# Two norm roots by way of ScalarE's Sqrt, one LoRA step instead of two, and token sums in parts, in a gated FFN with an S4 branch

## The chip, the core and the metric

The kernel runs on one core of a Trainium2 chip. A core has five engines that run their own instruction streams, each in order: TensorE (PE; its weight loads are listed as PEld), VectorE (DVE), ScalarE (ACT), GpSimd (POOL) and SyncE (SP), which here issues nearly all DMAs. Engines wait for one another by semaphores. SBUF is the working memory with 128 partitions, PSUM holds the results of TensorE in eight banks of 128x512 floats. The metric is the time of one execution on the device in microseconds (us): median of three runs, 442.49, from 442.27 to 443.13.

## The reference, cut to what matters

The input is x, 2 x 1024 tokens of 512 values. All is fp32.

```python
x = L0_attn_u                                   # (2, 1024, 512)
xn = _layernorm(x)                              # (x - mean) / sqrt(var + 1e-5)
s = S4(xn)                                      # a causal convolution along the 512 values of each token
g = silu(FFN(xn))                               # below
return x + s * g

# FFN, HID = 1376, R = 16, SCALING = 2
h1 = xn @ w1.T + (xn @ A1.T @ B1.T) * SCALING
h3 = xn @ w3.T + (xn @ A3.T @ B3.T) * SCALING
g  = silu(h1) * h3
out = g @ w2.T + (g @ A2.T @ B2.T) * SCALING
```

## The kernel before, in words

**Tiling.** The 2048 tokens are four blocks of 512 (`TB`), each of four tiles of 128 tokens (`NTT`); blocks 0 and 1 make "super block" 0, blocks 2 and 3 super block 1. A tile is normalized with tokens on the partitions, transposed on TensorE, and copied by ScalarE out of PSUM into `xr` and `b12`, with the 512 values (in four chunks of 128) on the partitions.

**Fast matrix products.** The first stage, h1 and h3, takes the 1376 hidden values in five pairs of 256 and a last chunk of 96 (`LAST`). w1 and w3 are first merged with their LoRA part, w + 2 B A: a product of 16 rows on TensorE (`lora_product`, L380) and an addition on VectorE (`merge`, L391). The stage is then a Strassen-Winograd product on two levels for the pairs and one level for the last chunk: seven products instead of eight per level, at the price of sums of weights and tokens. The outer sums of tokens are made by `outer_token_sum` (L328), those of weights by `outer_weight_sums` (L440); the inner ones by `inner_token_sum` (L340 makes T3, L342 T2, L344 T4, L346 T1) and `inner_weight_sum` (L452). Each inner token sum is made in two calls: `raw` over the three blocks of `xr`, 128x1536, and once over the four of `xt`, 128x2048. T2 builds on T3 and T4 on T2; T1 overwrites its operand.

**Chains.** `Chain` (L765) runs one set of seven products; `step(i)` issues product i (L755) into banks x, y or w of PSUM, and what follows it: the copy of x to w (L793), snapshots of x (L775), totals (L779). A pair's seven chains (`pair_chains`) have the inner index j = 1, 2, 6, 7, 5, 3, 4, and read T2 in j = 6 and T1 in j = 5 and T4 in j = 4. Their results are added up in `ua` and `u3` (L869), passed through Silu on ScalarE (L828), multiplied on GpSimd (L836) and stored to DRAM.

**Order of work.** The order on TensorE, VectorE, ScalarE and GpSimd is written out by hand. `at(place, what)` puts a step on a heap, `after(delay, what)` puts one behind the current place, and the heap is emptied in order of place; each engine executes its instructions in the order in which they were emitted. One unit of place is about one product. A chain's products stand at 7n plus the offsets of a table, such as `PLACES`. PSUM is given out by `bank(tag)`: x, y, w and aux have two banks each and take turns; with `borrow` the next bank is used without the turn passing.

**The start.** SP and ScalarE issue the loads of block 0; then come the LoRA factors for two row groups (`load_lora`, groups 0 and 1), block 1, the last chunk's weights, pair 0's weights, blocks 2 and 3, pair 1's weights, and the LoRA factors for groups 2 and 3. In the trace eight DMAs are under way at most: an issue starts once the one eight places ahead of it has landed. ScalarE loads the table for Silu with a dummy activation (L972). TensorE multiplies the identity by itself (`keep_warm`, L988) and makes the LoRA product of the last chunk. VectorE makes mean and variance of each tile (`norm_stats`, L247 and L248). `norm_root` (L278) adds EPS and calls `rsqrt` (L50), eight instructions on VectorE that begin with an integer guess, and makes the shift (L284); `normalize` applies both, two tiles on ScalarE (L293) and two on GpSimd (L297). Block 0 is transposed into the aux banks (L304), block 1 into the y banks. Block 3's sums are made by ScalarE (`act_sums`, `act_squares`), and one root serves blocks 2 and 3 (`norm_root(mv_late, 2, 3)`).

**LoRA of pair 0.** `merge_pair` (L407) takes half a pair at a time, four products with 16 rows in row groups 0 and 1, at places -9 and -3.8. The other pairs use `merge_whole_pair` (L418), eight products in four row groups and four banks, which needs the LoRA factors of groups 2 and 3.

After the first stage come the S4 matrix and the second stage, which the change does not touch.

Of the kernel before, what the change touches and what calls it, by code (L numbers as in the profile page):

```python
# [12 lines left out]
F32 = mybir.dt.float32  # L13
# [36 lines left out]
def rsqrt(nc, pool, v, shape):  # L50


    y = pool.tile(shape, F32, tag="rs_y", name="rs_y")
    t = pool.tile(shape, F32, tag="rs_t", name="rs_t")
    part = 3.0 / 8.0
    c2 = part * 0.703952253
    nc.vector.tensor_scalar(
        y.bitcast(I32), v.bitcast(I32), -0.5, float(0x5F1FFFF9), ALU.mult, ALU.add
    )
    nc.vector.tensor_tensor(t, y, y, ALU.mult)  # L60
    nc.vector.scalar_tensor_tensor(t, t, -c2, v, ALU.mult, ALU.mult)
# [46 lines left out]
def s4_gated_ffn(  # L108
# [110 lines left out]
    def after(delay, what):  # L219
        at(now[0] + delay, what)  # L220
# [54 lines left out]
            norms[b][:, :, 1], sums_of_x[b][:, 2, :], 1.0 / DIM, None, mult  # L275
        )

    def norm_root(mv, *blocks):  # L278
        n = len(blocks) * NTT
        veps = small.tile([P, n], F32, tag="veps", name="veps")  # L280
        nc.vector.tensor_scalar(veps, mv[:, :, 1], EPS, None, add)
        rstd = rsqrt(nc, small, veps, [P, n])
        shift = small.tile([P, n], F32, tag="shift", name="shift")
        nc.vector.scalar_tensor_tensor(shift, mv[:, :, 0], -1.0, rstd, mult, mult)  # L284
        for n, b in enumerate(blocks):
            norms[b] = [t[:, n * NTT : (n + 1) * NTT] for t in (rstd, shift)]
# [9 lines left out]
            else:  # L296
                nc.gpsimd.tensor_scalar(t, t, rstd[:, one], shift[:, one], mult, add)  # L297

    def transpose(b, tiles, tag="aux"):
        sb, low = divmod(b, 2)  # L300
        for tt in tiles:
            ps = bank(tag)
            for dc in range(NDC):
                nc.tensor.transpose(  # L304
                    ps[:, dc * P : (dc + 1) * P],
                    x_in[b][tt][:, dc * P : (dc + 1) * P],
                    ident,
                )
            at_ = slice(tt * P, (tt + 1) * P)
            halves = ps.rearrange("p (c k t) -> p c k t", c=2, k=2)  # L310
            if low == 0:
                nc.scalar.copy(xr[:, 0:2, sb, :, at_], halves)
            else:
                nc.scalar.copy(b12[sb][:, :, at_], halves[:, 0])
                nc.scalar.copy(xr[:, 2, sb, :, at_], halves[:, 1])
# [16 lines left out]
            nc.sync.dma_start(out=b12_dram[:, sb], in_=b12[sb])  # L332
        nc.sync.dma_start(out=i12_dram, in_=xr[:, :, 1, 0, :])

    def inner_token_sum(name, raw):
        src, lo, n = (xr, 0, 3) if raw else (xt, 3, 4)
        to = {i: t[:, lo : lo + n, :] for i, t in t_in.items()}
        b11, b21, b12_, b22 = (src[:, :, s, k, :] for s in range(2) for k in range(2))
        if name == 3:
            nc.vector.tensor_tensor(to[7], b22, b12_, sub)  # L340
        elif name == 2:
            nc.vector.tensor_tensor(to[6], to[7], b11, add)  # L342
        elif name == 4:
            nc.vector.tensor_tensor(to[4], b21, to[6], sub)  # L344
        else:
            nc.vector.tensor_tensor(b12_, b12_, b11, sub)  # L346
# [57 lines left out]
                )  # L404
        return w

    def merge_pair(c, w, half, tag="aux"):  # L407

        ps = [bank(tag), bank(tag)]
        for k in range(2):  # L410
            for v in range(2):
                n = slice(k * 2 * P, (k + 1) * 2 * P)
                lora_product(ps[v][:, n], v, 2 * half + k, PAIR_AT[c], 2 * P, k == 0)
        for v in range(2):
            to = w[:, (1, 2, 0, 3)[2 * v + half]].rearrange("p k m h -> p (k m h)")
            after(1.6 + v, lambda to=to, v=v: merge(to, ps[v]))

    def merge_whole_pair(c, w, first=None, delays=(1.15, 2.3, 4.3, 4.4)):  # L418

        ps = [first or [bank("y", True), bank("w", True)], [bank("aux"), bank("aux")]]  # L420
# [41 lines left out]
    def load_last():  # L462
        both = const.tile([P, 2, 2 * NDC * LASTR], F32, tag="w2b", name="last")
        w, s = (
            both[:, i].rearrange("p (a b h) -> p a b h", a=n, h=LASTR)
            for i, n in enumerate((2, 4))
        )
        for v, src in enumerate((w1T, w3T)):
            nc.sync.dma_start(
                out=w[:, v], in_=src[:, LAST * P :].rearrange("(dc p) h -> p dc h", p=P)  # L470
            )
        return w, s

    def lora_last():
        ps = [bank("y"), bank("y")]
# [487 lines left out]

    x_in = {0: load_x(0)}
    warm = const.tile([P, 1], F32, name="warm")
    nc.gpsimd.memset(warm, 0.0)
    make_identity(nc, ident)
    lora_tiles(LSPLIT)
    factors = (a1, b1T), (a3, b3T)
    for v, f in enumerate(factors):  # L970
        load_lora((nc.sync, nc.scalar)[v], v, *f, LSPLIT, HID)
    nc.scalar.activation(warm, warm, AF.Silu)  # L972
    x_in[1] = load_x(1)
    make_upper_triangular(nc, tri, 1.0, diag=True)
    w_last, s_last = load_last()
    w_pair, s_pair = {0: load_pair(0)}, {c: {} for c in range(NPAIR)}
    x_in[2], x_in[3] = load_x(2), load_x(3)
    w_pair[1] = load_pair(1)
    for v, f in enumerate(factors):
        load_lora(nc.sync, 2 + v, *f, LSPLIT, HID)  # L980

    def other_factors():
        for v, (_, h) in enumerate(factors):
# [18 lines left out]
    ps_last = lora_last()  # L1002
    mv = norm_tile(0)
    norm_stats(0, range(NTT))
    norm_root(mv, 0)
    normalize(0)

    keep_warm(primed[1], 4)
    transpose(0, range(NTT))
    mv = norm_tile(1)  # L1010
    norm_stats(1, range(2))
    merge_last(w_last, ps_last, 0)
    norm_stats(1, range(2, NTT))
    norm_root(mv, 1)
    merge_last(w_last, ps_last, 1)
    mv_late = norm_tile(2, 3)
    ab_last = last_operands(w_last, s_last)

# [37 lines left out]
            add_chain(2 + 7 * c + n, pair_chain(c, n), places)  # L1056
    at(-10, lambda: normalize(1))
    at(-9.9, lambda: last_sums(w_last, s_last))
    at(-9, lambda: merge_pair(0, w_pair[0], 0))
    at(-3.8, lambda: merge_pair(0, w_pair[0], 1))  # L1060
    for i in range(2):
        at(-6 + i, lambda i=i: transpose(1, range(2 * i, 2 * i + 2), "y"))
    for n, name in enumerate((3, 2, 1)):
        at((-2.3, -1.5, -0.45)[n], lambda name=name: outer_token_sum(0, name))
        at(-0.6 + 0.3 * n, lambda name=name: outer_weight_sums(w_pair[0], (name,)))
    at(0.4, lambda: outer_token_sum(0, 4))
    at(0.8, lambda: outer_weight_sums(w_pair[0], (4,)))
    for tt in range(NTT):
        at(-6 + 0.8 * tt, lambda tt=tt: norm_stats(2, (tt,)))
        at(-1.4 + 0.1 * tt, lambda tt=tt: act_sums(3, tt))  # L1070
        at((-0.3, -0.2, 1.7, 1.8)[tt], lambda tt=tt: act_squares(3, tt))
    at(-0.9, lambda: act_means(3))
    at(1.9, lambda: act_variances(3))
    at(6.9, lambda: norm_root(mv_late, 2, 3))
    at(7.3, lambda: normalize(2))
    at(7.7, lambda: normalize(3, (0,)))
    for n, place in enumerate((12.1, 12.8, 13.7, 14.4)):
        b, i = divmod(n, 2)
        at(place, lambda b=b, i=i: transpose(2 + b, range(2 * i, 2 * i + 2)))
# [3 lines left out]
    at(22.5, spill)  # L1083
    for name, when in ((1, 12.7), (2, 13.4), (4, 14), (3, 30.5)):
        at(when, lambda name=name: inner_weight_sum(w_pair[0], s_pair[0], name))
    for name, raw, when in (
        (3, True, 21.6),
        (2, True, 22.8),
        (3, False, 24.2),
        (2, False, 30.2),  # L1090
        (1, True, 34.4),
        (1, False, 37.5),
        (4, True, 43.3),
        (4, False, 47.6),
    ):
        at(when, lambda name=name, raw=raw: inner_token_sum(name, raw))

    for c in range(NPAIR):
        t0 = 14 + 49 * c
# [492 lines left out]
```

## Time and profile before

| what | value |
|---|---|
| median of 3 runs | 442.49 us (442.27 to 443.13) |
| profiled execution, its own time | 442.57 us |
| its span, first to last instruction | 440.8 us |
| busy TensorE / VectorE / GpSimd / ScalarE | 98% / 72% / 47% / 33% |
| mean granted TensorE clock | 0.998 |
| DMA | 53.61 MB, mean 122 GB/s |

The profile's page gives busy shares of each engine over the span, the span in 40 slices of 11 us with the busy share in tenths, and the chain of work that ended last: from the last instruction back, at each step to what released it. The timeline lists instructions in order of time: start, duration, engine, line, operation, output and inputs, and in brackets the idle time of the engine before it and what ended that. The ends of matrix products are modelled, so two that follow each other overlap in the list; the distance from start to start is what counts. Records with "x8" are several merged into one line.

### The profile page before, as it was taken

The page shows a single profiled execution, that of the slowest core. Times are in us where ns is not written, and L with a number is a line of the kernel's source. Part 1 is how long each engine was busy: PE and PEld are TensorE (multiplying, and loading weights), DVE is VectorE, ACT ScalarE, POOL GpSimd, SP SyncE. Part 2 cuts the span into 40 slices and gives each one's busy share as a digit, 9 for nine tenths or more (in the row PEclk, how much of TensorE's full clock was granted, in tenths as well). Part 3 has the DMA queues.
Part 4 walks back from the last instruction along what each step waited for, and adds up shares of the span by engine and source line. Part 5 has one row for each costly group of instructions (what it writes and reads, how often), then busy time and mean ns, then how long its engine had stood idle before and what let it go on. Part 6 is the DMA issues. An engine that isn't in the chain of part 4 may idle for free.

```text
span 440.8 us, 5156 instructions
## 1 busy us (share of the span) xinstructions
PE 433.5 (98%) x1704; PEld 268.5 (61%) x1704; DVE 316.9 (72%) x534; ACT 144.2 (33%) x296; POOL 209.3 (47%) x156
## 2 busy tenths in 40 slices
PE   7999999999999999999999999999999999999996
PEld 7545333444444444444443447888898999999995
DVE  5899999946974597469746796979786875753234
ACT  2777242453245324532453242211101212112221
POOL 2325469995689368936894469400000123222221
PEclk9999999999999999999999999999999999999999
DMA  8921304025002400350045526395902833423211
GB/s 258 370 66 47 116 0 149 24 72 168 25 24 96 143 24 25 99 160 24 25 148 187 167 90 214 112 348 200 342 22 75 306 115 95 144 97 95 88 57 48
DMA packets 35466, 53.61 MB, mean 122 GB/s; under 512 B 4688, under 2 KB 21520, under 8 KB 35312
## 3 DMA queue, kind: packets, MB, share of 16 engines
q1 hardware_dynamic: 35088, 52.69, 36.9%
q10 hardware_dynamic: 352, 0.60, 0.4%
q8 instruction: 13, 0.21, 0.2%
q14 instruction: 13, 0.11, 0.1%
HBM read 33.88 MB, written 19.40 MB: 121 GB/s over the span
## 4 chain that ended last, share of the span: by engine, by line
PE 84%; DVE 10%; issue 2%; ACT 2%; DMA 1%; POOL 0%; SPq 0%; DVEq 0%; POOLq 0%
PE x L755 42%; PE y L755 21%; PE w L755 11%; PE aux L929 4%; PE w L929 2%; DVE s L452 1%; DVE t_in L342 1%; DVE xt L328 1%; DMA s<-in_x_dram 1%; DVE t_in L340 1%; DVE w L440 1%; DVE s L779 1%; PE y L382 1%; PE y L528 1%; PE aux L710 1%
## 5 line engine op out<-in xcount | busy, mean ns | idle before, releaser
L1310 POOL TENSOR_TENSOR o<-o,xin 128x512 f32<-128x512 f32 (+1 forms) x17 | 23.3, 1369 | 132.9 <-DVE o L1309 132.9
L836 POOL TENSOR_TENSOR s<-c,s 128x512 f32<-128x512 f32 (+1 forms) x44 | 63.1, 1439 | 16.1 <-ACT c L828 10.9
L775 ACT COPY s<-x 128x512 f32<-128x512 f32 (+1 forms) x54 | 31.6, 584 | 86.8 <-PE x L755 86.7
L755 PE MATMUL x<-t_in,s 128*128 128x512 f32 (+1 forms) x148 | 55.4, 501 | 0.0
L779 DVE TENSOR_TENSOR s<-s,y 128x512 f32<-128x512 f32 (+1 forms) x54 | 36.0, 679 | 17.2 <-PE y L755 12.1
L869 POOL TENSOR_TENSOR s<-ua_three,s 128x512 f32<-128x512 f32 x20 | 35.9, 1793 | 25.7 <-DVE s L779 25.7
L755 PEld LDWEIGHTS x<-t_in,s 128*128 128x128 f32 x148 | 26.6, 190 | 23.3 <-issue 12.0
L869 POOL TENSOR_TENSOR ua_three<-ua_three,s 128x512 f32<-128x512 f32 x20 | 33.0, 1652 | 15.1 <-DVE s L779 15.1
L755 PE MATMUL y<-t_in,s 128*128 128x256 f32 (+1 forms) x108 | 35.8, 458 | 0.0
L1332 ACT COPY z<-x 128x256 f32<-128x256 f32 x24 | 8.8, 371 | 70.5 <-PE x L755 70.4
L1307 DVE TENSOR_TENSOR aux<-aux,m 128x384 f32<-128x384 f32 x32 | 18.1, 565 | 15.8 <-PE aux L929 14.3
L869 POOL TENSOR_TENSOR s<-u_three,s 128x512 f32<-128x512 f32 x20 | 28.5, 1430 | 1.8 <-ACT c L828 1.0
L828 ACT ACTIVATE c<-c 128x512 f32<-128x512 f32 x40 | 25.2, 632 | 10.0 <-DVE c L869 10.0
L755 PEld LDWEIGHTS y<-t_in,s 128*128 128x128 f32 x108 | 20.2, 190 | 11.1 <-issue 9.3
L793 ACT COPY w<-x 128x512 f32<-128x512 f32 (+1 forms) x37 | 21.1, 570 | 12.2 <-PE x L755 12.2
L869 POOL TENSOR_TENSOR u_three<-ua_three,u_three 128x512 f32<-128x512 f32 x10 | 15.6, 1557 | 11.6 <-DVE u_three L779 11.5
L755 PE MATMUL x<-t_in,w 128*128 128x512 f32 x40 | 20.9, 603 | 0.0
L755 PE MATMUL x<-xr,s 128*128 128x512 f32 x40 | 20.6, 616 | 0.2 <-DVE ua_one L869 0.2
L755 PE MATMUL x<-xt,w 128*128 128x512 f32 x40 | 20.7, 598 | 0.0
L755 PE MATMUL x<-xr,w 128*128 128x512 f32 x40 | 20.6, 614 | 0.0
L755 PE MATMUL x<-xt,s 128*128 128x512 f32 x40 | 20.4, 592 | 0.0
L440 DVE TENSOR_TENSOR w<-w 128x512 f32<-128x512 f32 x20 | 20.1, 1015 | 0.1
(302 smaller groups left out, 906.0 us busy)
## 6 DMA issues: line engine op xcount, KB each, us to landing
g_dram<-s SPq DMA_DIRECT2D x40, 256.0 KB, 2.1
g<-g_dram SPq DMA_DIRECT2D x10, 512.0 KB, 5.6
xin<-in_x_dram SPq DMA_DIRECT2D x16, 256.0 KB, 2.8
out_dram<-o SPq DMA_DIRECT2D x14, 256.0 KB, 2.0
t_in<-g_dram SPq DMA_DIRECT2D x6, 512.0 KB, 4.2
w<-in_w1T_dram SPq DMA_DIRECT2D x10, 256.0 KB, 3.3
w<-in_w3T_dram SPq DMA_DIRECT2D x10, 256.0 KB, 5.0
t_in<-in_x_dram SPq DMA_DIRECT2D x8, 256.0 KB, 5.5
```

The lines of the kernel that those rows point to most:

```text
L440: nc.vector.tensor_tensor(*sums[name])
L755: nc.tensor.matmul(ps[:, cols], lhsT=lhsT, rhs=rhs if parts == 1 else rhs[:, cols], start=first and i == 0 and part == 0, stop=i == len(pa ...
L775: nc.scalar.copy(t, self.x)
L779: nc.vector.tensor_tensor(t, t, self.y, add)
L793: nc.scalar.copy(self.w, self.x)
L828: nc.scalar.activation(c, c if src is None else src, AF.Silu)
L836: nc.gpsimd.tensor_tensor(g, act, g, mult)
L869: (nc.vector if o < 20 else nc.gpsimd).tensor_tensor(to, a, b, add)
L929: nc.tensor.matmul(to[:, n * P : (n + 1) * P], lhsT=x_, rhs=by, start=start, stop=True, skip_group_check=True,)
L1307: nc.vector.tensor_tensor(y[:, P:], y[:, P:], m[:, n * P : (n + 3) * P], add)
L1310: (nc.vector if last else nc.gpsimd).tensor_tensor(o, o, self.xin[h][:, cols], add)
L1332: nc.scalar.copy(t, xb)
```

## The change

1. `norm_root` can take its root by `refined`: ScalarE's Sqrt of variance plus EPS, VectorE's reciprocal, and one Newton step against the exact variance plus EPS. Blocks 0 and 1 use it; blocks 2 and 3 keep `rsqrt`. The dummy activation at the start is Sqrt; one of Silu follows the second root. The second merge of the last chunk goes ahead of block 1's root.
2. Pair 0's LoRA products are made by one `merge_whole_pair` at -9, in two y banks and two aux banks, with its four merges from 1.6 on; `merge_pair` goes. The factors of groups 2 and 3 are loaded ahead of pair 0's weights; the last chunk's first half is loaded ahead of block 1, its second half behind it.
3. Of block 1's transposes the first goes to a bank of x, the other three to y. Three of block 2's four statistics, and the normalization of blocks 2 and 3, move to later places. `keep_warm` makes five products instead of four.
4. T1's second call and T4's second call are split into halves of 128x1024, and T4's calls move later.

```diff
+    def refined(mv, veps):
+
+        shape = list(veps.shape)
+        y = small.tile(shape, F32, tag="rs_y", name="rs_y")
+        t = small.tile(shape, F32, tag="rs_t", name="rs_t")
+        root = small.tile(shape, F32, tag="root", name="root", bufs=1)
+        nc.scalar.activation(root, mv[:, :, 1], AF.Sqrt, bias=eps)
+        nc.vector.tensor_scalar(veps, mv[:, :, 1], EPS, None, add)
+        nc.vector.reciprocal(y, root)
+        nc.vector.tensor_tensor(t, y, y, mult)
+        nc.vector.scalar_tensor_tensor(t, t, -0.5, veps, mult, mult)
+        nc.vector.scalar_tensor_tensor(y, t, 1.5, y, add, mult)
+        return y
+
-    def norm_root(mv, *blocks):
+    def norm_root(mv, *blocks, on_act=False):
         n = len(blocks) * NTT
         veps = small.tile([P, n], F32, tag="veps", name="veps")
-        nc.vector.tensor_scalar(veps, mv[:, :, 1], EPS, None, add)
-        rstd = rsqrt(nc, small, veps, [P, n])
+        if on_act:
+            rstd = refined(mv, veps)
+        else:
+            nc.vector.tensor_scalar(veps, mv[:, :, 1], EPS, None, add)
+            rstd = rsqrt(nc, small, veps, [P, n])
...
-    def transpose(b, tiles, tag="aux"):
+    def transpose(b, tiles, tag="aux", borrow=False):
...
-            ps = bank(tag)
+            ps = bank(tag, borrow)
...
-    def inner_token_sum(name, raw):
+    def inner_token_sum(name, raw, half=None):
         src, lo, n = (xr, 0, 3) if raw else (xt, 3, 4)
-        to = {i: t[:, lo : lo + n, :] for i, t in t_in.items()}
-        b11, b21, b12_, b22 = (src[:, :, s, k, :] for s in range(2) for k in range(2))
+        some = slice(n) if half is None else slice(2 * half, 2 * half + 2)
+        to = {i: t[:, lo : lo + n, :][:, some] for i, t in t_in.items()}
+        b11, b21, b12_, b22 = (src[:, some, s, k, :] for s in range(2) for k in range(2))
...
-    nc.gpsimd.memset(warm, 0.0)
+    eps = const.tile([P, 1], F32, name="eps")
+    for t, v in ((warm, 0.0), (eps, EPS)):
+        nc.gpsimd.memset(t, v)
...
-    nc.scalar.activation(warm, warm, AF.Silu)
+    nc.scalar.activation(warm, warm, AF.Sqrt)
+    w_last, s_last, load_of_last = load_last()
+    load_of_last(0)
     x_in[1] = load_x(1)
+    load_of_last(1)
     make_upper_triangular(nc, tri, 1.0, diag=True)
-    w_last, s_last = load_last()
+    for v, f in enumerate(factors):
+        load_lora(nc.sync, 2 + v, *f, LSPLIT, HID)
     w_pair, s_pair = {0: load_pair(0)}, {c: {} for c in range(NPAIR)}
     x_in[2], x_in[3] = load_x(2), load_x(3)
     w_pair[1] = load_pair(1)
-    for v, f in enumerate(factors):
-        load_lora(nc.sync, 2 + v, *f, LSPLIT, HID)
...
-    norm_root(mv, 0)
+    norm_root(mv, 0, on_act=True)
     normalize(0)
 
-    keep_warm(primed[1], 4)
+    keep_warm(primed[1], 5)
     transpose(0, range(NTT))
     mv = norm_tile(1)
     norm_stats(1, range(2))
     merge_last(w_last, ps_last, 0)
     norm_stats(1, range(2, NTT))
-    norm_root(mv, 1)
     merge_last(w_last, ps_last, 1)
+    norm_root(mv, 1, on_act=True)
+    nc.scalar.activation(warm, warm, AF.Silu)
...
-    at(-9, lambda: merge_pair(0, w_pair[0], 0))
-    at(-3.8, lambda: merge_pair(0, w_pair[0], 1))
-    for i in range(2):
-        at(-6 + i, lambda i=i: transpose(1, range(2 * i, 2 * i + 2), "y"))
+    at(
+        -9,
+        lambda: merge_whole_pair(
+            0, w_pair[0], [bank("y"), bank("y")], (1.6, 1.7, 1.8, 1.9)
+        ),
+    )
+    at(-6, lambda: transpose(1, (0,), "x", True))
+    at(-5.9, lambda: transpose(1, range(1, NTT), "y"))
...
-        at(-6 + 0.8 * tt, lambda tt=tt: norm_stats(2, (tt,)))
+        at((-6, 0.84, 0.85, 0.9)[tt], lambda tt=tt: norm_stats(2, (tt,)))
...
-    at(7.3, lambda: normalize(2))
-    at(7.7, lambda: normalize(3, (0,)))
+    at(7.7, lambda: normalize(2))
+    at(7.75, lambda: normalize(3, (0,)))
...
-        (1, False, 37.5),
-        (4, True, 43.3),
-        (4, False, 47.6),
+        (1, False, 37.5, 0),
+        (1, False, 40.3, 1),
+        (4, True, 47.6),
+        (4, False, 50.2, 0),
+        (4, False, 52.3, 1),
     ):
-        at(when, lambda name=name, raw=raw: inner_token_sum(name, raw))
+        at(when, lambda of=(name, raw, *half): inner_token_sum(*of))
```

More of the change, by code (lines that the diff above doesn't have):

```diff
@@ L405, in load_pair @@
         return w
[L407 to L416, printed above, removed]
     def merge_whole_pair(c, w, first=None, delays=(1.15, 2.3, 4.3, 4.4)):
@@ L467, in load_last, with load @@
         )
-        for v, src in enumerate((w1T, w3T)):
+        def load(v):
             nc.sync.dma_start(
-                out=w[:, v], in_=src[:, LAST * P :].rearrange("(dc p) h -> p dc h", p=P)
+                out=w[:, v],
+                in_=(w1T, w3T)[v][:, LAST * P :].rearrange("(dc p) h -> p dc h", p=P),
             )
-        return w, s
+        return w, s, load
     def lora_last():
@@ L1085, in s4_gated_ffn @@
         at(when, lambda name=name: inner_weight_sum(w_pair[0], s_pair[0], name))
-    for name, raw, when in (
+    for name, raw, when, *half in (
         (3, True, 21.6),
```

## The prediction

> **What bounds the kernel now.** I read the page first: busy shares, slices, chain.
>
> ```profile
> PE 433.5 (98%) x1704; PEld 268.5 (61%) x1704; DVE 316.9 (72%) x534; ACT 144.2 (33%) x296; POOL 209.3 (47%) x156
> ...
> PE   7999999999999999999999999999999999999996
> PEld 7545333444444444444443447888898999999995
> DVE  5899999946974597469746796979786875753234
> ...
> PE 84%; DVE 10%; issue 2%; ACT 2%; DMA 1%; POOL 0%; SPq 0%; DVEq 0%; POOLq 0%
> ```
>
> TensorE is the bound: only its first and last slices are below nine. A product of 128x512 is two records, 0.43 us apart in steady state, so 0.86 us each; what the change can win is TensorE work dropped, and places where that step is longer. VectorE is full in slices 3 to 8 (22 to 88 us) and carries 10% of the chain. So I read the chain in order of time, then the timeline, for who holds whom there.
>
> ```profile
> 58.86 2.20 DVE t_in L342
> 61.06 1.00 DVE s L452
> 62.66 2.15 DVE xr L346
> 65.41 1.28 DVE xt L346
> ```
>
> ```profile
> 61.12 0.30 PEld L755 LDWEIGHTS x<-t_in,s 128*128 128x128 f32 x2 [0.73 <-DVE t_in L342]
> ...
> 68.17 1.02 PE L755 MATMUL x<-t_in,s 128*128 128x512 f32 x2
> ...
> 69.35 0.30 PEld L755 LDWEIGHTS x<-xr,s 128*128 128x128 f32 x2 [0.98 <-DVE ua_one L869]
> ...
> 72.89 1.02 PE L755 MATMUL w<-xr,s 128*128 128x512 f32 x2
> ...
> 73.95 0.30 PEld L755 LDWEIGHTS y<-xt,s 128*128 128x128 f32 x2 [0.87 <-DVE s L779]
> ```
>
> The reader is to see a "lock" at 55.5 and 61.1: the products of T2 start the moment VectorE has made T2 (L342 ends at 54.87 and 61.06), and TensorE arrives just then. If TensorE came earlier it would wait; if VectorE comes later, so does everything. Then two stalls. The product of 68.17 has its successor due at 69.03; it comes at 69.35 and takes 0.10 longer (1.12 for 1.02, its weights not loaded ahead): 0.42 lost behind a sum (L869) that was queued behind T1 in one piece (L346, 65.34 to 68.10). After 72.89 the successor is due at 73.75 and comes at 73.95: 0.30 lost, with the same 0.10, behind a total (L779) that was queued behind T4 (L344, 70.46 to 73.30).
>
> The start, from the timeline:
>
> ```profile
> 2.59 1.28 ACT L972 ACT_TABLE_LOAD   x1 [2.59 <-issue]
> ...
> 20.91 1.13 PE L382 MATMUL aux<-lo_h,lo_d 16*128 16x256 f32 x8
> 20.99 1.29 DVE L328 TENSOR_TENSOR xt<-xr,b 128x512 f32<-128x512 f32 x2 [0.64 <-ACT xr L315]
> ```
>
> A table load costs ScalarE 1.28 us; half of pair 0's LoRA costs TensorE 1.06 (20.91 to 21.97); and block 2's statistics, before L328, ran partly in time in which VectorE waits for block 1's transposes anyhow.
>
> **The change, part by part.**
>
> First root. Before: ten small VectorE instructions from 7.60 to 9.54, one each 0.196, then ScalarE normalizes at 9.58 and transposes start at 10.44. After: Sqrt on ScalarE, then reciprocal, product, two fused steps, shift; the EPS add runs beside Sqrt. No Sqrt is in the trace: below, a 128x1 ACTIVATE is 0.20; above, a 128x512 one with a bias operand 0.72. The size is that of the small one; the bias operand adds about 0.10 (0.72 against 0.62 for the copies of act_sums), so 0.30. The 128x4 reciprocal at L668 took 0.178. With hand-overs of 0.04: 7.60 + 0.30 + 0.04 = 7.94, reciprocal to 8.12, four steps of 0.196 to 8.90. That is 0.64 earlier, and 0.22 at the upper bound. Queued behind the waiting reciprocal are block 1's statistics, wanted no sooner than their tiles land. The fifth keep_warm adds two records of 0.11, the last issued at 9.54, within the wait that ends at 9.80; uncovered they cost 0.22. The memset of eps (0.10 on GpSimd) delays only warm-up products that precede a wait for DMA until 7.23.
>
> Loads. One half of the last chunk's weights now precedes x1 on SP's queue: it took 0.71 (landings 9.72 to 10.43), so x1's tiles land at about 8.3, 9.0, 9.7, 10.4 and are read at 8.8, 9.7, 10.9, 11.7. Four LoRA loads (0.33 of issue each, 0.80 from first to last landing) pass the sixteen loads of pair 0, blocks 2 and 3 and pair 1: pair 0 lands by 15.4 instead of 14.6, needed at 15.8; block 2's first tile at 16.0, needed at 17.7; pair 1 at 24.6, needed at 32. So nothing, with 0.4 us in hand; a later landing would be paid one for one.
>
> Second root. Sqrt stands behind the copies of block 0's transposes on ScalarE (13.61 before, 12.97 now): it ends at 13.2, the shift at 14.3 instead of 15.21 (behind the waiting reciprocal stand pair 0's merges, which wait for the LoRA products until 15.2 anyhow). But ScalarE then loads Silu's table: 1.28 + 0.20 as at 2.59, so to 14.72, ahead of the copy L793, for which x is ready at 14.13. L793 thus starts 0.08 earlier instead of 0.64. Waiting behind the load: L793, on which the next product hangs, and the normalization of block 1 (15.2, needed at 17.1). TensorE does the whole pair's LoRA (16 records, 1.07 as at 29.92) from 14.06 to 15.13, waits until 15.35, and comes to block 1's transposes at 17.14 instead of 17.55.
>
> Here the Trainium skill speaks against the change (ScalarE: Activation LUTs, "What ACT_TABLE_LOAD costs" and the rule to batch calls by table set): a switch costs some 2.66 us, a drain of about 1.38 included. This trace's single load, on an idle engine, took 1.28 and the ACTIVATE began 0.01 after it. By the page L793 would start near 16.1 and my sum below would be about 1.4 higher.
>
> Transposes of block 1. Tile 0 goes to a bank of x, the other three alternate in y; now the fourth instead of the third waits for a copy, about 0.45 either way. Copies end at 20.36 (the Silu of L828, 0.63, now stands behind them), so L328 starts at 20.39 instead of 20.99. TensorE is at the last chunk's y product at 20.4, since the second LoRA group (1.06 at 20.91) is gone, but the first half of L328 ends at 21.08: it starts at 21.15 instead of 21.97. TensorE is 0.8 ahead.
>
> VectorE from there to the lock. Before: L328 at 20.99, fourteen operations at 0.60, root at 29.61. After: two merges fewer (they ran in the new gap before 17.8), but three of block 2's four statistics come in (L247 and L248, 2.47 for three; before, they stood at 17.88 to 20.34, beside waits). 20.39 + 12 x 0.60 + 2.47 gives the root at 30.12: 0.51 later. The 0.23 that L779 waits for ScalarE's snapshot at 33.65 goes, since normalize now follows that snapshot. VectorE is 0.28 later at 34 and full until 61. Then T2 ends 0.28 later, and TensorE's lead of 0.8 becomes a wait of 1.1 at 55.5. Bounds: GpSimd's sums (L836 at 35.43, 39.44, L869 at 48.13) stretch L452 to 2.19, L440 to 1.65, L342 to 2.64, about one us each over their neighbours; one such meeting less or more moves the lock by 1.0. So +0.28 between -0.8 (TensorE's own lead) and +1.3.
>
> T1 and T4 in parts. A half of 128x1024 is about 1.2, from 1.08 at 896 columns and 2.28 at 2048; a split costs 0.15. With half of T1 and T4's first part gone from ahead of L869 and L779, these come 1 to 2 us earlier than wanted, and the two stalls go: -0.42 and -0.30. What is late next: behind the sums of 47.2 (before, 75.0) now stands T4's first part, then L779, L452, L779, the first half of T4's second part, and the two L869 that free a bank of x (81.80 before; the product that wants it stood at 82.72, and by the sum below it will stand at 82.3). Bare: 75.05 + 1.74 + 0.6 + 1.5 + 0.6 + 1.2 + 1.2 = 81.9. With GpSimd in the way of both parts (2.84 as at 70.46, and 1.7): 83.5. So a new stall of 0 to 1.2. I take 0, since the part of T4 that stood in that slot before was not stretched (2.31 at 75.61, as 2.28 at 55.39).
>
> Sum: 442.57 (the profiled execution; span 440.8) + 0.28 - 0.42 - 0.30 = 442.13; the median is 0.08 below that execution, so 442.05, say 442.0.
>
> **Rivals.**
>
> The lead passes (440.9): if one meeting with GpSimd falls away between 35 and 61, VectorE no longer holds the lock and TensorE's 0.8 arrives: 442.49 - 0.8 - 0.72 = 441.0, with 0.1 for the step at 55.0. For: these meetings depend on tenths. Against: VectorE has 0.1 of idle time there and the same order.
>
> T4 in its new place (443.4): if GpSimd's sums meet both T4's first part and its first half, L869 ends at 83.5: 442.05 + 1.2 = 443.25, and 0.1 for a second split. It decides from 82.3 on. For: GpSimd is 9 tenths busy there. Against: VectorE gained 0.5 before it.
>
> The roots do nothing for the time (442.6): the second table load takes 1.9 or more, so that L328 is not earlier than before; the lock then stands at 0.28 + 0.60 = 0.88, and 442.49 + 0.88 - 0.72 = 442.65. For: L793 has no slack, and a later load is paid one for one. Against: the row at 2.59.
>
> **How the numbers follow.** A measurement of this kernel tells about 0.2%, 0.9 us, from no change. Forecast, 441.4 to 442.9: 0.45, of it 0.40 within that bound and 0.05 faster. The lead passes: 0.35, all faster. T4: 0.14, slower. No use of the roots: 0.06, of it 0.04 within, 0.02 slower. So faster 0.40, same 0.44, slower 0.16. The range takes in the first rival's end, 440.8, and most of the second's, 443.2.
>
> **What would show it.** Right: block 0's transposes at 9.8; one table load of 1.28 near 13.3 and L793 near 14.7; one group of 16 L382 records before 16; the y product near 21.15; the late root near 30.1; waits for L342 at 55 and 61 that grew to about 1 us; steps of 0.86 from 68 to 75. Wrong: T2 ready before 60.6 (the first rival), a wait for L869 near 82 (the second), L793 after 15.2 (the third), or a wait for pair 0's weights at L392.

## The result, and the profile after

The changed kernel takes 443.43 us (median of 15 executions, 442.45 to 445.14) against 442.49 for the kernel before in the same comparison (15 executions, 442.08 to 443.88): ratio 1.0019, 95% interval 1.0012 to 1.0027. The forecast was 442.0 in a range of 440.8 to 443.2; by the ratio the change costs 0.8 us (the medians lie 0.9 apart) instead of gaining 0.5. The profiled execution took 443.19, its span is 441.3 (before 442.57 and 440.8).

From the page of the kernel after, busy shares, slices and the chain by engine:

```profile
PE 433.4 (98%) x1706; PEld 269.2 (61%) x1706; DVE 315.3 (71%) x528; ACT 146.3 (33%) x300; POOL 209.9 (48%) x157
...
PE   8899999999999999999999999999999999999996
PEld 8545334344444444444443446888898999999996
DVE  4799999964984688458746796979786885654234
...
PE 85%; DVE 9%; DMA 4%; ACT 1%; issue 0%; SPq 0%; ACTq 0%; DVEq 0%
```

TensorE is busy for the same 433 us, and VectorE is full in the same slices. New is DMA with 4% of the chain (before 1%). The chain in order of time (start, duration, what) shows where that DMA stands, and what follows from it:

```profile
7.02 6.47 DMA last<-in_w3T_dram
...
13.51 5.28 DMA w<-in_w3T_dram
...
18.91 0.70 DVE w L410
19.61 0.14 issue
19.75 0.64 PE y L321 x4
...
21.65 2.50 DVE xt L345 x4
...
31.48 0.18 DVE veps L298
...
53.80 2.64 DVE t_in L360
56.44 0.61 DVE c L879
```

The last chunk's second half lands at 13.50 (before 11.62). An issue starts once the load eight places ahead has landed (in the trace the loads take eight semaphores in turn; that is how this program waits, and no run shows a limit of the hardware). So the last load of pair 0 is issued at 13.51 and lands at 18.79 (before 14.57). Pair 0's merge (L410) waits for it in a bank of y, block 1's transposes wait for that bank, and VectorE's row of outer sums (L345) begins at 21.65 instead of 20.99, where the forecast had 20.39. From there the chain stays on VectorE, with pauses of about 0.5 us at most, through the late root (the one of blocks 2 and 3, L298) to T2 (L360) and the sum behind it (L879), for which T2's first product waits. Instructions of ScalarE, VectorE and TensorE of the kernel after, in the timeline's columns (start, duration, engine, line, operation; in brackets the idle time before and what ended it):

```profile
14.02 0.30 ACT L284 ACTIVATE root<-mv,eps 128x4 f32<-128x4 f32 x1 [0.73 <-DVE mv L248]
14.34 1.28 ACT L1030 ACT_TABLE_LOAD   x1
15.63 0.20 ACT L1030 ACTIVATE warm<-warm 128x1 f32<-128x1 f32 x1
15.74 0.57 ACT L803 COPY w<-x 96x512 f32<-96x512 f32 x1
...
18.91 0.69 DVE L410 SCALAR_TENSOR_TENSOR w<-y,w 128x512 f32<-128x512 f32 x1 [2.67 <-DMA w<-in_w3T_dram]
...
57.09 0.30 PEld L765 LDWEIGHTS x<-t_in,s 128*128 128x128 f32 x2 [1.23 <-DVE c L879]
62.68 0.30 PEld L765 LDWEIGHTS x<-t_in,s 128*128 128x128 f32 x2 [0.73 <-DVE t_in L360]
...
69.74 1.02 PE L765 MATMUL x<-t_in,s 128*128 128x512 f32 x2
70.60 1.02 PE L765 MATMUL x<-xr,s 128*128 128x512 f32 x2
...
74.03 1.02 PE L765 MATMUL w<-xr,s 128*128 128x512 f32 x2
74.89 1.02 PE L765 MATMUL y<-xt,s 128*128 128x512 f32 x2
...
83.65 0.30 PEld L765 LDWEIGHTS x<-t_in,w 128*128 128x128 f32 x2 [0.76 <-DVE c L879]
```

T2's second product has its weights at 62.68 (before 61.12). The two stalls are gone: from 69.74 to 70.60 and from 74.03 to 74.89 the step is 0.86. At 83.65 there is a small new wait, for the sums (L879) behind T4's first half. Start of the same product, before and after:

| where | before | after | later by |
|---|---|---|---|
| the last chunk's y product | 21.97 | 22.49 | 0.52 |
| T2's product | 55.52 | 57.09 | 1.57 |
| behind the first stall | 69.35 | 70.60 | 1.25 |
| behind the second stall | 73.95 | 74.89 | 0.94 |
| behind T4's new place | 83.58 | 84.79 | 1.21 |
| TensorE's last product ends | 436.52 | 437.76 | 1.24 |
| span | 440.76 | 441.32 | 0.56 |

The last two rows differ because before's profiled execution took 4.24 from TensorE's last product to its end; after took 3.56, and eleven of the twelve profiles of the experiments 3.54 to 3.58 (the other 3.80). That execution was long there by 0.68.

### The profile page after: what moved, and what is told of

Same layout as the page of the kernel before. It is cut to its first block, busy times and chain, and to the rows that moved or that the text cites. A ratio compares the mean times of both kernels' runs of the same rounds, so it can differ in the third digit from the quotient of the medians.

```text
span 441.3 us, 5162 instructions
## 1 busy us (share of the span) xinstructions
PE 433.4 (98%) x1706; PEld 269.2 (61%) x1706; DVE 315.3 (71%) x528; ACT 146.3 (33%) x300; POOL 209.9 (48%) x157
## 4 chain that ended last, share of the span: by engine, by line
PE 85%; DVE 9%; DMA 4%; ACT 1%; issue 0%; SPq 0%; ACTq 0%; DVEq 0%
PE x L765 43%; PE y L765 22%; PE w L765 11%; PE aux L939 4%; PE w L939 2%; DVE xt L345 2%; DMA last<-in_w3T_dram 1%; DVE w L447 1%; DMA w<-in_w3T_dram 1%; DMA s<-in_x_dram 1%; DVE s L459 1%; PE y L400 1%; PE y L538 1%; PE aux L720 1%; DVE w L410 1%; DVE t_in L360 1%
## 5 line engine op out<-in xcount | busy, mean ns | idle before, releaser
L785 ACT COPY s<-x 128x512 f32<-128x512 f32 (+1 forms) x54 | 31.5, 584 | 85.2 <-PE x L765 85.1
L879 POOL TENSOR_TENSOR s<-ua_three,s 128x512 f32<-128x512 f32 x20 | 35.8, 1791 | 26.7 <-DVE s L789 26.7
L789 DVE TENSOR_TENSOR s<-s,y 128x512 f32<-128x512 f32 (+1 forms) x54 | 36.0, 678 | 16.2 <-PE y L765 10.2
L879 POOL TENSOR_TENSOR ua_three<-ua_three,s 128x512 f32<-128x512 f32 x20 | 30.6, 1531 | 12.8 <-DVE s L789 12.8
L879 POOL TENSOR_TENSOR s<-u_three,s 128x512 f32<-128x512 f32 x20 | 29.4, 1474 | 1.8 <-ACT c L838 1.0
L803 ACT COPY w<-x 128x512 f32<-128x512 f32 (+1 forms) x37 | 21.2, 572 | 9.7 <-PE x L765 9.5
L879 POOL TENSOR_TENSOR u_three<-ua_three,u_three 128x512 f32<-128x512 f32 x10 | 15.6, 1557 | 14.4 <-DVE u_three L789 14.3
L765 PE MATMUL y<-xt,w 128*128 128x512 f32 x40 | 19.8, 592 | 0.0
```

Of the source, the lines that this page charges most:

```text
L765: nc.tensor.matmul(ps[:, cols], lhsT=lhsT, rhs=rhs if parts == 1 else rhs[:, cols], start=first and i == 0 and part == 0, stop=i == len(pa ...
L785: nc.scalar.copy(t, self.x)
L789: nc.vector.tensor_tensor(t, t, self.y, add)
L803: nc.scalar.copy(self.w, self.x)
L879: (nc.vector if o < 20 else nc.gpsimd).tensor_tensor(to, a, b, add)
```

## The experiments

There were three theories of the loss. *Load order*: the last chunk's first half, now ahead of block 1, and the four LoRA loads make everything behind them late. *Row of sums*: three of block 2's statistics, put between the outer sums and the late root, hold T2. *Lock-out*: GpSimd is kept out while VectorE works; this one came from the second profile of after, below. Rival to all: the roots or T1 and T4 in parts cost what is lost. All medians stand beside runs of the kernel before on the same chip.

### One part alone, and after once more

parts_only is the kernel before with T1 and T4 in parts; roots_only has the two roots by Sqrt alone; lora_only is the kernel after with roots and T1, T4 as before, so the loads, the whole-pair LoRA, the transposes, the statistics and the normalization at their new places are left. after_again is the kernel after, run once more. The edits are cut to the lines that matter.

```diff
parts_only, on before
-        (1, False, 37.5),
-        (4, True, 43.3),
-        (4, False, 47.6),
+        (1, False, 37.5, 0),
+        (1, False, 40.3, 1),
+        (4, True, 47.6),
+        (4, False, 50.2, 0),
+        (4, False, 52.3, 1),
...
roots_only, on before
-    norm_root(mv, 0)
+    norm_root(mv, 0, on_act=True)
...
-    norm_root(mv, 1)
+    norm_root(mv, 1, on_act=True)
+    nc.scalar.activation(warm, warm, AF.Silu)
```

> The kernel before with T1 and T4 in parts at the new places, nothing else. If the two stalls behind L346 and L344 are worth what their steps say (0.42 + 0.30 us) and nothing takes their place: 441.8 against 442.5. If the sums behind T4's first half come late near 82 us, as my second rival has it: 442.5 or more, with a wait for L869 there.

> The kernel before with the first two roots by Sqrt, the table for Silu loaded after the second, and the fifth keep_warm. By my sum VectorE loses eight small instructions and TensorE is 0.4 us earlier at block 1's transposes, the T2 products at 61.1 come about 0.4 earlier: 442.1. If the second table load is the cause of the loss (a wait of L793 longer than the 0.64 us won ahead of it): 443.0 or more.

> The changed kernel with the roots and T1 and T4 as before: what is left are the loads in their new order, pair 0's LoRA in one step, block 1's transposes, block 2's statistics and normalize at their new places. Theory of the loads: block 1's tiles and pair 0's last quarter land late, VectorE waits for them and T2 is some 1.5 to 2 us later than in the kernel before: 444.0, with a wait for a load ahead of one of pair 0's merges. Theory of the statistics: the loads are in time and only the three statistics behind L328 push VectorE: 443.0, and no wait for a load. If both are harmless, TensorE's 1.06 us of LoRA products is won: 441.5.

> The changed kernel once more, for a second trace. If the late landings in its first trace (block 1's second tile 2.6 us after the first, pair 0's last quarter 2.7 us after the third) come from the order of the loads, they are there again at the same DMAs, within some tenths. If they were a disturbance of that one execution, this trace has landings some 0.7 us apart and a span shorter by a microsecond. Time 443.4.

| kernel | median | before | ratio, interval |
|---|---|---|---|
| parts_only | 442.39 | 442.59 | 0.9993 (0.9984 to 1.0002) |
| roots_only | 442.33 | 442.59 | 0.9994 (0.9986 to 1.0002) |
| lora_only | 443.31 | 442.59 | 1.0022 (1.0010 to 1.0033) |
| after_again | 442.97 (up to 447.86) | 442.59 | 1.0016 (1.0000 to 1.0032) |

Roots and parts don't cost; neither alone is told from no change. The loss is in lora_only. The late landings came back in after_again: block 1's second tile lands 2.1 us behind the first, pair 0's last load at 17.80. So they belong to the order of the loads and not to one execution. In four of the five profiles with that order the second tile lands 1.7 to 2.6 us behind the first, in the ten other profiles 0.7; why it is so isn't known.

The profiles of lora_only and after_again show a wait that the first one of after lacks: TensorE stands 2.67 us, at 28 us. Before's row, and the chain of after_again:

```profile
24.00 0.68 DVE L392 SCALAR_TENSOR_TENSOR w<-aux,w 128x512 f32<-128x512 f32 x1
24.15 0.22 POOL L260 TENSOR_SCALAR act_sums<-act_sums 128x4 f32<-128x4 f32 x1 [4.99 <-ACT c L254]
```

```profile
24.83 0.73 ACT c L254 x2
...
25.64 3.52 POOL act_sums L260
...
29.18 1.52 ACT c L265 x4
30.70 0.48 ACT s L785
...
31.31 2.44 PE x L765 x4
```

A small operation of GpSimd, 128x4 (0.22 in before), takes 3.51. ScalarE's squares (L265) wait for it, the snapshot of x (L785) stands behind the squares on ScalarE, and TensorE's next product waits for the snapshot. From 21.75 to 28.98 VectorE runs only sums of two operands in SBUF (L345, L447). In before, L260 ran at 24.15 for 0.22, beside a merge, which reads PSUM (0.22 to 0.23 in all four profiles that have the merges there); the change moved the merges out of the row. L260 also took 2.68 in lora_only and 0.30 in the first profile of after, so it doesn't strike each time: in that profile L260 got in between two sums. That became the theory *lock-out*.

### The lock-out and the load order, crossed

holes puts two of the statistics, which read one operand, between the sums. last_behind moves the last chunk's first half back behind block 1. holes_last does both. roots_parts is the kernel before with both roots and parts.

```diff
holes
-        at((-6, 0.84, 0.85, 0.9)[tt], lambda tt=tt: norm_stats(2, (tt,)))
+        at((-6, -0.4, 0.1, 0.9)[tt], lambda tt=tt: norm_stats(2, (tt,)))
last_behind
-    load_of_last(0)
     x_in[1] = load_x(1)
+    load_of_last(0)
     load_of_last(1)
```

> The kernel after, with two of block 2's four statistics (L247, L248) moved forward into VectorE's row of sums: one behind the outer sum that ended at 25.87, one behind the two weight sums that follow. The amount of VectorE work is the same. Theory 'GpSimd is locked out': GpSimd's 128x4 operation at L260 can't start while VectorE reads two operands of SBUF without a break, and a statistic (one operand) lets it in. Then L260 takes under 1.3 us in the profile, the wait of TensorE ahead of x<-xt,last at 28 us (2.67 in the second profile of after) is under 0.3, and no run lies more than 1 us above the median. The late loads stay, so the median stays between 442.7 and 443.4 (ratio 1.0005 to 1.0020). Rival 'block 3 lands too late': the wait comes from x3's landing and ScalarE's sums, L260 is just the row where it shows; then the wait of 2 us and more returns and the spread is that of after (2.7 us over 15 runs).

> The kernel after, with the first half of the last chunk's weights back behind the four tiles of x1 on SP's queue; the LoRA loads stay where after has them. Theory 'the load order': x1's last tile lands before 10.2 (12.87 in after), pair 0's last half before 16.2 (18.79), VectorE waits under 0.5 for pair 0's weights (2.67), the first outer sum starts before 20.7 (21.65) and the late root before 30.5 (31.48); T2 of 62.63 comes about 1 us earlier. If the lock-out of GpSimd does not strike, 442.2 to 442.6 (ratio 0.9993 to 1.0003); if it does, 2.5 more in those runs, and the spread stays wide. Rival 'VectorE's order' (statistics of block 2 behind the sums cost by themselves what after lost): the loads land early but the late root stays after 31 and the ratio at or above 1.0012.

> Both edits at once: load of the last chunk's first half behind x1, and two statistics of block 2 between the sums. If the two theories (load order, lock-out of GpSimd) are the whole loss, this is what the change was predicted to be: 441.9 to 442.4, ratio 0.9987 to 0.9998, all runs within 1 us of the median, first outer sum before 20.7, late root near 30.1, T2 near 61.3, no gap of TensorE above 1.2 us after 22 us. If something third is at work, the ratio stays above 1.0005.

> The kernel before with two parts of the change alone: the first two roots by Sqrt (with the table load behind the second), and T1 and T4 in parts at the new places. Loads, LoRA, transposes and statistics as before. Apart they gave 442.33 and 442.39 against 442.59. Theory 'they add': 442.1, ratio 0.9987 to 0.9991, both stalls of 68 to 75 us gone and the first outer sum no later than 21.0. Rival 'VectorE holds the time at T2 and at 82 us': what the roots win of TensorE's lead is waited away, ratio 0.9993 as each alone.

| kernel | median | before | ratio, interval |
|---|---|---|---|
| holes | 443.23 (442.46 to 443.58) | 442.63 | 1.0010 (1.0001 to 1.0018) |
| last_behind | 445.11 (443.40 to 447.17) | 442.63 | 1.0059 (1.0036 to 1.0081) |
| holes_last | 443.02 (442.29 to 444.26) | 442.63 | 1.0008 (0.9997 to 1.0020) |
| roots_parts | 442.28 (441.60 to 443.52) | 442.63 | 0.9997 (0.9988 to 1.0007) |

last_behind (6 executions) and holes_last (11) differ by the two statistics alone: 2.1 us. The timeline of last_behind:

```profile
25.48 3.89 POOL L260 TENSOR_SCALAR act_sums<-act_sums 128x4 f32<-128x4 f32 x1 [5.68 <-ACT c L254]
...
28.60 0.69 DVE L447 TENSOR_TENSOR w<-w 128x512 f32<-128x512 f32 x1
29.20 0.69 DVE L247 BATCH_NORM_STATS2 stats<-t_in 128x6 f32<-128x512 f32 x1
...
29.40 0.72 ACT L265 ACTIVATE c<-t_in,act_sums 128x512 f32<-128x512 f32 x1 [3.19 <-POOL act_sums L260]
...
31.53 3.43 PE L765 MATMUL x<-xt,last 128*96 128x512 f32 x4 [2.51 <-ACT s L785]
```

and of holes:

```profile
24.18 0.88 POOL L260 TENSOR_SCALAR act_sums<-act_sums 128x4 f32<-128x4 f32 x1 [5.68 <-ACT c L254]
...
24.90 0.69 DVE L247 BATCH_NORM_STATS2 stats<-t_in 128x6 f32<-128x512 f32 x1
```

L260 ends at 29.37 and 25.06, 0.17 and 0.16 after a statistic has begun (29.20 and 24.90). So it is the first instruction with one operand that lets GpSimd in. The lock-out is shown, and holes did as expected: no execution lies more than 0.35 above its median. It is not the whole loss: holes is still slower than before, and holes_last, which was to be all that the change had promised (441.9 to 442.4), is at 443.02. So a third thing is at work.

The load order fell as the cause of the median's loss. last_behind and holes_last did bring loads forward: over the five profiles with each order, pair 0's last load lands at 16.1 on average instead of 17.4, block 2's first tile at 16.9 instead of 18.9. But the first outer sum begins at 21.2 against 21.4, and holes and holes_last differ by 0.2 us, within their intervals. In last_behind it began at 21.97: the last chunk's halves landed at 12.18 and 13.39 there too, and L260 became ready inside the unbroken row. roots_parts tells its two expectations not apart: its interval holds both. In its profile, with the loads as before has them, the last chunk's second half landed at 12.71, the first outer sum began at 21.95 and TensorE ended 1.0 later than in before. So a late start costs in the execution in which it falls, and it falls with either order.

### The row of sums

In holes_last VectorE is idle from 18.78 to 20.69, waiting for the copies of block 1's transposes, and the late root starts at 30.52. early2 puts the second statistic into that idle time, early3 the second and third; early2_t4 is early2 with both halves of T4's second part behind the sums (L879) that free a bank; stats3 is the kernel after with early3's statistics, its loads as they were.

```diff
early2, on holes_last
-        at((-6, -0.4, 0.1, 0.9)[tt], lambda tt=tt: norm_stats(2, (tt,)))
+        at((-6, -5.2, -0.4, 0.1)[tt], lambda tt=tt: norm_stats(2, (tt,)))
early3, on holes_last; stats3, on after
+        at((-6, -5.2, -4.4, -0.4)[tt], lambda tt=tt: norm_stats(2, (tt,)))
early2_t4, on early2
-        (4, False, 50.2, 0),
+        (4, False, 52.25, 0),
```

> The kernel holes_last with one more of block 2's four statistics moved: the second one now stands with the first, ahead of the outer sums, in time in which VectorE waits for block 1's transposes anyhow (18.78 to 20.69 in holes_last); the last two stay between the sums. Theory 'VectorE's row holds the lock at T2': 0.86 of VectorE work leaves the row between the first outer sum and the late root, so the late root starts at 29.7 (30.52 in holes_last), T2 ends near 61.3 less 0.8, and TensorE comes to T2's first product at 55.4 instead of 56.1; 442.3 as median (443.02 for holes_last), ratio 0.9987 to 0.9996. Rival 'the loss lies in the loads alone': T2 moves, but the runs vary with the landing of loads as before and the median stays at 442.9 to 443.2.

> As early2, with three statistics ahead of the outer sums and one between them. The third tile of block 2 landed at 19.17 in holes_last and at 19.67 in holes, so its statistic ends at 20.05 to 20.55, and the first outer sum, due at 20.69, is not held by more than 0.3. Late root at 28.9; T2's products at 54.6 to 54.9 if nothing else holds them; 441.9 as median, ratio 0.9977 to 0.9990. Rival 'block 2 lands late': where its third tile lands at 20.3 or later, as in the run of the loads and the LoRA alone, the first outer sum is late by as much, and nothing is won over early2.

> As early2, with the first half of T4's second part moved behind the two sums (L879) that free a bank of x, so that both halves stand together. Theory 'T4 in its new place': in holes_last the product x<-t_in,w waited for that sum at 82.69, and from 74 to 87 us TensorE fell back by 0.39 against before. With the sums 1.6 earlier that wait goes: the gap ahead of x<-t_in,w at 82 us falls from 0.11 to under 0.05 and the fall-back from 0.39 to under 0.2; 0.1 to 0.3 below early2. Rival 'T4 is wanted there': the product that reads the first half waits instead, with a gap of 0.3 or more between 82 and 84 us, and nothing is won.

> The kernel after with the statistics as early3 has them (three of block 2 ahead of the outer sums, one between them) and the loads left as after has them. It tells what the order of the loads is worth by itself, once VectorE's row of sums is short and broken. Theory 'the row of sums was the loss': T2's products come at 54.9 to 55.8 without a wait of 0.5, and the time is that of early3, 441.7 to 442.2, ratio 0.9975 to 0.9990. Rival 'the load order is half of it': pair 0 and block 2 land 1 to 2 us later than in early3, the first outer sum waits for the third statistic to 22 or later, T2 is at 56 to 57, and the time is 442.5 to 443.2 (ratio 0.9999 to 1.0015).

| kernel | median | before | ratio, interval |
|---|---|---|---|
| early2 | 442.22 | 442.55 | 0.9989 (0.9975 to 1.0003) |
| early3 | 441.89 | 442.55 | 0.9980 (0.9966 to 0.9994) |
| early2_t4 | 443.22 | 442.55 | 1.0017 (1.0002 to 1.0031) |
| stats3 | 441.71 | 442.45 | 0.9989 (0.9973 to 1.0005) |

early3 differs from holes_last by the places of three statistics, and neither profile has a lock-out: 1.1 us between the medians, with intervals that don't meet. That is the row of sums. stats3 differs from after in the same way, and the loss is gone, though its loads keep after's order: pair 0's last lands at 17.51 (18.79 and 17.80 in after's two profiles), and the first outer sum begins later than in after's first profile. Its statistic in the row lets L260 in as well (1.16), so of the step from 1.0019 to 0.9989 a part is the lock-out; holes, which removes that alone, is at 1.0010. The rival that the load order is half of the loss (442.5 to 443.2) fails. The chain of stats3:

```profile
13.69 3.81 DMA w<-in_w3T_dram
...
20.34 0.59 DVE stats L247
...
21.13 0.59 DVE stats L247
...
21.92 0.59 DVE xt L345
22.51 0.14 issue
22.65 1.93 PE y L765 x4
24.57 0.86 PE w L765 x2
```

From 22.65 to beyond 75 nothing but TensorE stands in it: VectorE's row no longer sets the time. The row from the first outer sum to the late root and T2's end, in five of the profiles without a lock-out of 2 us and more:

| kernel | first outer sum | late root | row | T2 ends |
|---|---|---|---|---|
| before | 20.99 | 29.61 | 8.62 | 61.07 |
| after | 21.65 | 31.48 | 9.83 | 62.63 |
| holes_last | 20.69 | 30.52 | 9.83 | 61.66 |
| early3 | 21.26 | 29.49 | 8.23 | 60.50 |
| stats3 | 21.84 | 30.03 | 8.19 | 61.04 |

early3 is the one kernel whose interval lies below 1: 0.2% faster than before. T2's first part is ready at 54.30, before TensorE asks for it; the weights of that product in its timeline stand without a wait:

```profile
54.95 0.19 PEld L765 LDWEIGHTS x<-t_in,s 128*128 128x128 f32 x1 [0.27 <-DVE c L879]
55.37 0.19 PEld L765 LDWEIGHTS x<-t_in,s 128*128 128x128 f32 x1 [0.24 <-issue]
```

early2_t4 missed, in a way neither theory had. With both halves in a row they take longer, and the total behind them (L789) frees its bank of y late:

```profile
80.00 3.94 DVE L362 TENSOR_TENSOR t_in<-xt,t_in 128x1024 f32<-128x1024 f32 x2
...
86.67 0.30 PEld L765 LDWEIGHTS y<-t_in,w 128*128 128x128 f32 x2 [2.17 <-DVE s L789]
```

The two halves take 3.94 against 1.69 and 1.21 in holes_last, and TensorE loses 1.5 us against early2. GpSimd works beside them in each of these profiles; that it is what stretches them was not tested. The change's own place for T4's halves was the better one.

## Why the prediction was wrong, step by step

The step that failed is the term "+0.28" of the sum, the lane of VectorE to T2. It measured +1.56 in the profile, and its three parts say where:

| part, against before | forecast | after | holes_last |
|---|---|---|---|
| start of the first outer sum | -0.60 | +0.66 | -0.30 |
| row to the late root | +1.11 | +1.21 | +1.21 |
| from there to T2's end | -0.23 | -0.31 | -0.32 |
| sum | +0.28 | +1.56 | +0.59 |

The length of the row was right; the lead that was to pay for three statistics in it never came. In the ten profiles with pair 0's LoRA in one step the first outer sum begins at 20.68 to 21.97, in none at the forecast 20.39. The runs showed what stands in its place: with the statistics beside a wait the loss is gone whichever way the loads stand (stats3, early3), and a lock-out of GpSimd, for which the sum has no term, comes on top in some executions. The steps in order:

- **First root**, forecast 0.64 earlier: right. Sqrt took 0.30, normalization starts at 8.83 instead of 9.58. Of this only 0.25 reached the transposes (10.19). They stood behind TensorE's own warm-up products: the step from one of their records to the next fell from 0.21 to 0.11 at 6.25 instead of 5.16, so the last chunk's LoRA product came at 7.91 instead of 7.37, and the fifth keep_warm, uncovered, cost its 0.22.
- **Loads**, "So nothing, with 0.4 us in hand; a later landing would be paid one for one": wrong as to the landing, which made the start late in this profile. Block 1's last tile landed at 12.87 instead of 10.4, pair 0 at 18.79 instead of 15.4, block 2's first tile at 19.46 instead of 16.0. I moved each load by the length of the one that passed it, and left out that with eight under way one late landing holds the issue eight places behind: the four LoRA loads put pair 0's last load eight places behind the last chunk's second half. In the median this is not the loss: holes and holes_last, with the two orders, differ by 0.2 us.
- **Second root**: the mechanism right. The load of the table took 1.28 and the ACTIVATE followed at once (15.63), here and in every other profile; the copy L803 came at 15.74, 1.0 late, as block 1 had landed late. The drain of 1.38 that the Trainium skill adds (ScalarE: Activation LUTs, "What ACT_TABLE_LOAD costs") is not seen in any run here. roots_only, at 0.9994, speaks against the rival in which the roots do nothing but hold L793 up: it is not slower.
- **Transposes and the first outer sum**, 20.39: came at 21.65, because the third tile waited for pair 0's merge in y, which waited for the load.
- **VectorE lane**: the row's length was right (20.39 to 30.12 is 9.73; measured 9.83; the terms as written, 20.39 + 7.20 + 2.47, give 30.06), its start 1.26 late. T2 at 62.63 instead of 61.34 is this. The bounds of -0.8 to +1.3 counted meetings with GpSimd and no late start.
- **T1 and T4 in parts**: both stalls went, -0.63 from T2's product to 73.95 in the table above instead of -0.72. "I take 0" for the new stall: it was 0.27 in after and 0.28 to 0.39 in holes_last by 84 and 87 us. Alone, the parts won 0.2 at the median (parts_only, not told from nothing), not 0.72: in that profile TensorE gains 0.62 up to 73.95 and has lost 0.39 of it by 100 us.
- **Rivals**. "The lead passes" needed T2 before 60.6: early3 is that case (60.50, and 441.89, not the rival's 440.9), once the row was short. "T4 in its new place" named a time, 443.4, that was nearly met, but its mechanism gave 0.4 of the 1.2, so that was luck. No rival had GpSimd kept out of the row: I counted GpSimd only as what stretches VectorE, and did not ask what the merges, taken out of the row, had let through.

For the profiled execution: 442.57 + 1.57 (T2) - 0.63 (stalls) + 0.30 (T4 and after) - 0.68 (the end, long in before's) = 443.13, measured 443.19. The lock-out comes on top in some executions: in the second profile of after TensorE is 3.2 late behind the wait at 31 us, 6.5 late at 39 us, since its clock fell (below), and 5.1 to 5.9 late from 62 us to the end.

What stays open: holes_last has a median of 443.02 and a profiled execution of 442.29, and which wait the others have isn't known. One is seen in holes: a weight load issued at 101.12 landed at 106.06 (before: 3.16 after its issue), and TensorE lost 1.0 us there: a product due at 106.04 came at 106.93 and took 0.10 longer. Nor can it be said in how many of after's executions the lock-out struck; two of them were profiled.

## What to carry to other kernels

Work that looks free to move must be counted in the row that it enters: statistics of 0.8 us each cost nothing beside a wait, and two more of them between sums that TensorE needs on time cost 1.1 us (443.02 in holes_last against 441.89 in early3). When operations are taken out of an engine's row, ask also what they let through: here two merges that read PSUM were the door through which a small instruction of another engine passed. Where a program keeps a limited number of loads under way, eight here, a load is held by the landing of the one eight places ahead of it, and not only by the sizes before it.

## What was unexpected of the hardware

- **GpSimd kept out.** A 128x4 operation took 2.68, 3.51 and 3.89 us beside unbroken VectorE sums with two operands in SBUF, and ended each time 0.17 after the next statistic had begun; it took 0.88 in the five kernels with a statistic at about 25 us, and 1.16 in stats3. The Trainium skill (SBUF — State Buffer, "Who interferes with whom", and "SBUF: two separate sides" for the length) says that such VectorE instructions and GpSimd's reads exclude one another, for the whole of an instruction. The runs agree on the exclusion; beyond it, GpSimd was not let in between one sum and the next, four to six times in a row, though it was once (0.30, in the first profile of after).
- **The clock after a wait.** Behind the 2.67 us wait of TensorE the granted clock fell in two of the three profiles that have this wait. The windows of after_again (us; busy time and instructions of PE, PEld, DVE, ACT, POOL; granted clock; DMA share; GB/s):

```profile
28.00:32.00 4.00, 1.50 (x4) 0.41 (x3) 3.37 (x8) 2.82 (x8) 1.34 (x2) 1.00 0.01 2
33.00:39.00 6.00, 6.00 (x21) 2.56 (x21) 4.05 (x14) 1.83 (x4) 3.79 (x5) 0.50 0.12 33
40.00:44.00 4.00, 4.00 (x16) 2.05 (x15) 3.96 (x5) 2.23 (x5) 1.29 (x1) 1.00 0.16 45
```

  It stood at 0.50 for about 7 us there (0.80 and 0.79 in the windows from 32 to 33 and 39 to 40), at 0.50 from 32 to 35 in last_behind, and at 1.00 in lora_only with the same wait; no other profile has such a wait behind the start, or such a fall. So a wait of this length can cost as much again: 3.2 us late against before became 6.5 in after_again, and 3.4 became 5.1 in last_behind.
- **The start of the full clock varies.** The warm-up products' records go from a step of 0.21 us to one of 0.11 at 4.5 us in the earliest of the fourteen profiles and at 7.7 in the latest (5.16 in before, 6.25 in after), with the same products from 1.4 us on. Among the profiles with the first root by Sqrt block 0's transposes came at 9.99 to 10.84, and the three latest of them (early2, early3, roots_only) are the three in which the step fell last.
- **Landings vary by more than is at stake.** The last chunk's second half landed at 11.3 to 11.6 in before, parts_only and roots_only, and at 12.7 in roots_parts with the same order of loads; in the ten profiles with the LoRA loads ahead of pair 0 it landed at 12.1 to 13.8.
